# Two routing groups of 12 and 4 sequences instead of 10 and 6, in a new written-out order

## The chip, the cores and the metric

The kernel runs on one core of a Trainium2 chip. The metric is device time in microseconds for one launch. The core has TensorE (PE: matmuls; PEld: its weight loads), VectorE (DVE), ScalarE (ACT), GpSimd (POOL) and SyncE (SP), each working through its own queue in order. SyncE's queue issues most DMA transfers; GpSimd issues the indirect ones, whose rows go to computed addresses.

## The reference

One transformer layer on 16 sequences of 256 tokens, 128 values each, in float32. Attention has 16 heads of 8 values; the feed-forward layer has 8 experts, of which each token uses its best two.

```
qkv = x @ w_qkv;  Q, K = rope(Q), rope(K)
out = softmax(causal(Q @ K^T * 8**-0.5)) @ V            # 16 heads of 8
x   = layernorm(x + out @ w_proj + b_proj)
logits = x @ W_router + b_router;  best two per token, softmax over the two
for e in range(8):
    y = relu(x @ W1[e] + b1[e]) @ W2[e] + b2[e]          # 128 -> 512 -> 128
    final += y * w[:, e]                                 # 0 where e is not among the two
x   = layernorm(x + final)
```

## The kernel before, in words

**Recording and order.** The kernel first records operations ("ops"), each with its engine, the ops it waits for, and the tiles it holds. Then `Plan.emit` issues them in the order of the list `ORDER`, a written-out permutation of the ops' numbers. Because every engine works through its queue in order, this list fixes which instruction waits behind which on each engine, and on SyncE's and GpSimd's DMA queues too. It only has to respect the dependences. The costs and ranks that ops carry are not used once the list is there.

**Attention, one sequence at a time** (`attention`, sixteen of them, in the list interleaved with one another). TensorE transposes x (L780), makes Q and K with and without swapped halves (L793) and V together with a part of the router's logits (L838). VectorE applies the rotation (L802, L803, L810). ScalarE masks Q by head (L822). TensorE computes scores in three pieces (L871), into one PSUM buffer; ScalarE takes the exponential of each piece (L896, 1.88 us); GpSimd sets what is not causal to zero (L881, "mask", 1.1 us for two of them and 2.05 us for the third); TensorE multiplies by V (L912, "weighing", four ops: two long, two short). ScalarE copies the result (L925); the denominators go out by DMA, are inverted on VectorE (L938) and come back spread over the partitions; VectorE scales (L956); TensorE projects (L966, with the rest of the logits); VectorE adds x (L978) and takes the moments (L745, L746). Each pair of sequences is then normalized (ScalarE L752, L753; VectorE L757 to L759 and L996).

**Routing by chunks.** `CHUNKS` is a list of groups, each a list of chunks, each a number of sequences in their order. When a chunk's last sequence is normalized, `route` runs once for it: VectorE finishes the logits (L1077 to L1080) and picks the two best experts (L1067 to L1071, L1087 to L1090); TensorE counts, with two matmuls, how many tokens each expert has (L1096, L1097, "count"); ScalarE and VectorE make the weights (L1118, L1122 to L1125); VectorE turns counts into places (L1102 to L1112, "places"). Then GpSimd scatters the chunk's rows to these places in DRAM (`rows`), one indirect DMA per 128 tokens for the first expert and one for the second (L1140, "scatter"), so four per sequence; before the second half it writes new destinations (L1129, L1136). A chunk's places are computed from those of the chunk before in the same group.

**Expert blocks by groups.** When all chunks of a group have places, `finish` computes on VectorE how many blocks of 128 rows each expert has (L1191 to L1250), and SyncE pads the ends (L1042). Blocks of one expert's rows are then processed (`block`), either pairs of 256 rows or singles of 128. With T tiles of 128 tokens in the group there are T - 7 pairs, and 19 singles are run. A block loads its expert's first matrix (L1311, 256 KB) and its rows (L1315, 65 KB per 128 rows; the load waits for every scatter of the group), transposes the rows (L1323), copies them (L1332), multiplies (L1339), applies bias and ReLU on ScalarE (L1352), multiplies by the second matrix (L1360), adds the bias (L1370) and multiplies by the row's weight (L1379); GpSimd sends each 128 rows to their token's place in DRAM (`back`, L1387, "send").

**Combining.** When all blocks of a group are sent, `combine` fetches each sequence's two results (L1472, 256 KB), adds them, normalizes, and stores 128 KB (L1547). For the first group VectorE adds (L1488, L1489) and ScalarE scales (L1506). For the last group TensorE adds into PSUM (L1455, L1478) and GpSimd takes the inverse square root (L1496, L1497). Twelve matmuls that nothing reads (L1557) run on TensorE while the last group's sends land.

**Around the change.** Before, the groups have 10 sequences (chunks of 4, 4 and 2) and 6 (one chunk). Sequences are numbered from 0, chunks are numbered from 0 through both groups. Sequence 9 closes chunk 2 and sequence 15 closes chunk 3.

Of the kernel before, what the change touches and what calls it, by code (L numbers as in the profile page):

```python
# [287 lines left out]

CHUNKS = [[4, 4, 2], [6]]

WARM = 12

# [14 lines left out]


ORDER = """
7 0 45 46 1 14 47 9 15 12 2 11 50 29 81 6 3 4 22 10 13 48 49 5 82 51 52 24 56 54 53 86 17 21 19
23 87 30 57 93 55 59 94 16 58 88 18 60 20 25 83 121 65 31 61 26 157 84 85 122 123 124 91 66 89
68 158 44 90 62 92 63 159 160 161 126 32 95 96 125 127 197 128 162 133 132 64 163 131 98 69 99
67 198 70 71 8 97 130 72 33 101 104 129 102 100 164 233 169 103 234 134 73 74 141 75 142 166
105 106 107 108 135 143 167 136 27 109 76 170 202 203 204 168 28 110 138 165 139 199 111 137
144 209 656 200 201 140 208 112 171 145 206 146 147 172 655 77 148 177 173 149 113 178 78 150
179 151 238 79 210 239 207 174 152 34 205 80 175 114 653 176 235 180 658 115 116 236 211 237
117 118 240 212 181 182 183 184 185 153 186 35 244 245 214 243 215 187 188 213 273 120 119 220
154 657 217 216 242 155 274 246 278 279 659 275 276 241 218 250 219 280 251 277 221 309 310 281  # L320
284 189 222 223 247 282 190 248 311 156 252 224 249 191 192 193 253 37 285 225 256 314 283 254
286 312 290 194 195 196 664 313 291 226 255 315 316 257 385 386 665 258 662 227 259 260 261 293
666 36 390 391 392 318 317 294 319 320 667 672 670 287 262 671 228 288 654 387 668 295 263 349
321 292 322 669 388 389 289 350 326 678 296 297 298 327 264 680 229 673 395 323 324 328 679 299
300 265 301 394 354 355 351 352 329 302 353 230 356 325 231 393 232 332 303 396 330 405 661 333
406 38 674 675 676 331 357 266 267 358 360 399 334 335 400 336 425 677 41 268 361 304 397 337
338 339 426 340 407 402 398 362 359 401 427 537 681 403 686 269 430 538 366 408 305 367 428 429
431 404 409 410 432 434 685 270 363 435 688 364 411 271 306 682 436 433 542 369 341 307 412 413
308 543 370 342 684 368 539 544 343 344 540 549 42 442 365 372 373 371 374 541 345 443 414 663
546 346 347 272 348 545 415 39 375 416 439 690 550 376 577 377 691 692 378 379 548 440 689 444  # L330
437 438 461 547 578 445 683 694 462 695 446 441 693 463 448 698 417 380 696 697 687 447 554 418
703 464 555 702 465 419 381 420 706 699 551 43 552 466 467 468 556 469 470 579 382 449 383 471
384 421 705 580 700 557 422 450 451 558 582 583 472 452 581 481 482 613 584 589 590 553 453 614
560 478 40 561 704 479 423 587 615 701 475 424 454 716 717 718 720 721 719 559 483 588 616 455
722 707 713 723 734 735 480 712 739 501 476 738 586 742 585 477 724 725 456 727 728 562 563 617
660 564 597 743 744 618 473 565 737 619 620 598 591 745 746 747 474 484 485 592 709 711 726 593
710 486 487 978 566 567 594 502 488 506 621 489 507 595 508 624 596 729 715 623 457 568 490 491
503 622 762 775 630 504 505 631 736 492 510 512 708 731 732 730 599 714 748 600 625 626 601 513
627 628 458 633 511 602 741 509 634 569 740 603 604 733 605 493 518 570 514 571 572 629 632 749
494 635 519 459 515 516 636 637 638 639 460 606 776 517 763 979 520 607 495 496 497 640 641 521  # L340
929 777 778 498 522 608 524 980 779 780 981 642 523 500 643 782 982 525 750 499 781 609 526 527
930 983 528 931 783 784 785 764 610 928 644 765 611 767 529 530 645 531 769 893 612 932 933 766
532 646 934 647 648 880 879 768 787 935 649 892 751 752 984 985 986 969 786 770 936 650 652 533
754 534 771 756 651 772 894 535 536 987 573 881 773 753 895 897 814 882 574 576 575 1189 968
815 1190 896 755 899 774 898 757 758 867 900 759 883 1191 901 1192 1193 1194 937 1195 760 761
902 1197 884 866 903 1196 904 1223 1225 885 886 887 1226 888 889 868 1199 1201 1208 840 869 841
890 1205 891 816 970 971 972 973 1228 817 1232 1233 1234 939 1188 789 1209 819 818 974 975 821
938 820 976 1029 788 1207 977 1202 1227 1204 870 872 1019 871 1230 949 822 873 1198 874 842 823
824 875 876 877 825 826 843 1028 940 878 1030 941 1031 1505 845 847 844 1018 790 846 942 943
791 793 795 1200 1206 848 948 906 849 792 944 945 905 850 794 1049 946 1032 1020 852 1203 851  # L350
1033 1021 1048 796 797 798 947 950 1022 1023 988 951 989 952 953 799 800 1235 1034 1506 907
1035 1024 908 1050 1051 918 1025 1036 954 909 1037 1210 910 1089 919 1026 955 911 1214 1027
1088 1236 959 912 990 991 956 1052 957 1008 1212 913 914 1090 1009 1053 1054 1091 915 920 921
1217 1055 992 1092 993 922 1553 1056 994 995 958 917 802 916 1093 923 1094 1095 996 1096 801
1231 960 961 924 1010 962 925 926 1011 803 804 1012 1078 963 964 1222 1057 965 1237 854 1013
1508 853 1229 966 997 1213 1079 1220 1097 1221 805 806 807 855 808 998 1069 927 856 1014 1015
858 809 860 999 1080 857 1016 1224 1211 810 1218 1070 1081 1068 828 859 811 1017 967 1071 1082
827 1000 1083 861 1038 1001 862 1002 1072 812 813 1084 1058 1085 1039 1098 863 1003 1215 1004
1073 1005 829 865 830 1059 1099 1086 1074 1216 864 831 1075 1076 833 1006 1040 832 1219 1041
1042 1100 1393 834 1101 835 836 1043 1087 1060 1102 1061 1251 1062 837 1044 1077 1252 1007 1103  # L360
1104 1253 1063 1045 1394 1105 1064 1277 1254 838 1046 1484 1106 839 1065 1066 1255 1395 1278
1396 1257 1256 1047 1397 1483 1554 1485 1067 1374 1486 1258 1259 1107 1555 1398 1373 1265 1172
1156 1279 1280 1260 1399 1487 1264 1261 1263 1400 1401 1488 1281 1375 1282 1354 1376 1239 1132
1266 1262 1489 1267 1353 1283 1173 1140 1402 1490 1157 1174 1158 1238 1284 1491 1334 1148 1377
1492 1378 1333 1285 1286 1175 1268 1355 1159 1270 1176 1356 1177 1269 1271 1160 1343 1287 1364
1161 1379 1178 1179 1240 1288 1357 1289 1358 1162 1241 1380 1381 1141 1363 1142 1272 1273 1344
1143 1335 1242 1274 1244 1382 1133 1164 1243 1245 1336 1144 1290 1276 1291 1275 1145 1146 1359
1360 1361 1314 1365 1108 1366 1337 1134 1313 1362 1338 1246 1147 1149 1247 1135 1345 1248 1367
1163 1346 1368 1136 1137 1138 1424 1249 1339 1347 1150 1348 1292 1369 1340 1293 1295 1250 1341
1370 1371 1423 1180 1342 1151 1315 1165 1464 1316 1297 1463 1152 1153 1294 1296 1166 1154 1324  # L370
1323 1167 1349 1350 1425 1317 1351 1426 1318 1155 1414 1109 1298 1299 1372 1352 1465 1466 1168
1427 1413 1300 1110 1428 1433 1139 1301 1434 1319 1320 1325 1467 1169 1326 1429 1302 1321 1327
1415 1303 1322 1430 1468 1304 1431 1416 1453 1454 1328 1469 1432 1170 1417 1470 1471 1404 1472
1435 1436 1418 1403 1329 1330 1331 1332 1474 1181 1437 1305 1306 1438 1473 1182 1111 1419 1307
1183 1308 1420 1421 1455 1444 1456 1184 1439 1405 1457 1185 1458 1440 1441 1406 1443 1383 1384
1171 1112 1442 1113 1114 1309 1407 1115 1475 1116 1310 1476 1459 1408 1477 1460 1422 1461 1311
1445 1446 1462 1478 1409 1410 1411 1447 1448 1385 1124 1386 1479 1480 1481 1387 1388 1449 1389
1493 1509 1312 1494 1495 1412 1482 1450 1496 1497 1498 1499 1500 1390 1451 1186 1117 1510 1391
1187 1452 1501 1502 1392 1525 1503 1504 1507 1526 1539 1118 1125 1126 1119 1120 1127 1128 1546
1532 1540 1121 1122 1123 1129 1527 1528 1547 1541 1529 1542 1533 1130 1511 1512 1548 1549 1530  # L380
1543 1534 1544 1550 1535 1131 1518 1531 1551 1545 1519 1552 1513 1536 1520 1537 1514 1538 1515
1516 1517 1521 1522 1523 1524
"""


class Held:

    def __init__(self, pool, tag, shape, dtype, bufs):  # L390
# [64 lines left out]
def main_path(  # L455
# [24 lines left out]
    HW = HEADS // 2  # L480
    ROUTED = CHUNKS
    TC = max(max(g) for g in ROUTED) * NT
# [1192 lines left out]
```

## Time and profile before

| | |
|---|---|
| three timed runs | 379.85 us median (376.16, 379.85, 381.21) |
| profiled execution | 373.53 us, span 372.1 us, TensorE clock 0.981 |
| TensorE busy | 332.6 us (89%) |
| ScalarE, GpSimd, VectorE busy | 252.3, 218.0, 202.6 us |
| DMA | 46.5 MB, 125 GB/s over the span |
| counts of the four chunks on TensorE | first at 78.7, last at 213.2 us |
| first transpose of block rows | 185.28 us |
| last expert matmul ends | 349.55 us |

The profile is of one execution, with times from the start of its span. A line of a timeline gives start, length, engine, source line, operation, tiles, and in brackets how long the engine was idle before it and what released it. Granted clock is the share of TensorE's full speed that it was given in a stretch.

### The profile page before, as it was taken

The page shows a single profiled execution, that of the slowest core. Times are in us where ns is not written, and L with a number is a line of the kernel's source. Part 1 is how long each engine was busy: PE and PEld are TensorE (multiplying, and loading weights), DVE is VectorE, ACT ScalarE, POOL GpSimd, SP SyncE. Part 2 cuts the span into 40 slices and gives each one's busy share as a digit, 9 for nine tenths or more (in the row PEclk, how much of TensorE's full clock was granted, in tenths as well). Part 3 has the DMA queues.
Part 4 walks back from the last instruction along what each step waited for, and adds up shares of the span by engine and source line. Part 5 has one row for each costly group of instructions (what it writes and reads, how often), then busy time and mean ns, then how long its engine had stood idle before and what let it go on. Part 6 is the DMA issues. An engine that isn't in the chain of part 4 may idle for free.

```text
span 372.1 us, 9773 instructions
## 1 busy us (share of the span) xinstructions
PE 332.6 (89%) x2960; PEld 246.6 (66%) x2960; DVE 202.6 (54%) x731; ACT 252.3 (68%) x547; POOL 218.0 (59%) x252
## 2 busy tenths in 40 slices
PE   5999999979999696797999887999999899989980
PEld 3554555545566353444589767999898899989960
DVE  3440566786368879854567872143321267635551
ACT  2889778878788665677655453666666489978642
POOL 5155343446887489488822567777777446553632
PEclk9999999999999999699999999899999999999997
DMA  4100354131321221165345436665765687776472
GB/s 127 44 3 13 113 75 118 32 102 62 118 63 55 74 59 40 31 154 171 87 114 152 132 93 170 162 187 155 218 196 156 178 249 237 231 204 194 142 213 76
DMA packets 53098, 46.51 MB, mean 125 GB/s; under 512 B 14610, under 2 KB 39577, under 8 KB 53042
## 3 DMA queue, kind: packets, MB, share of 16 engines
q1 hardware_dynamic: 48626, 37.36, 37.5%
q0 software_dynamic: 4416, 8.47, 6.8%
q8 instruction: 27, 0.44, 0.5%
q14 instruction: 29, 0.24, 0.2%
HBM read 33.53 MB, written 12.67 MB: 124 GB/s over the span
## 4 chain that ended last, share of the span: by engine, by line
PE 55%; DVE 16%; ACT 11%; DMA 6%; issue 5%; POOL 4%; ACTq 0%; DVEq 0%; POOLq 0%; SPq 0%
PE m L1339 14%; PE m L1360 13%; PE sc L871 8%; PE ps_o L912 7%; ACT pr L896 7%; PE m L793 4%; PE m L966 3%; POOL rows L1140 2%; DMA rows_in<-rows 2%; DVE lg L1079 2%; DVE x_sb L996 2%; POOL pr L881 2%; PE ps_o L1557 1%; DMA out_dram<-yout 1%; PE m L1323 1%
## 5 line engine op out<-in xcount | busy, mean ns | idle before, releaser
L896 ACT ACTIVATE pr<-sc 128x2048 f32<-128x2048 f32 x48 | 90.1, 1877 | 26.8 <-PE sc L871 24.9
L1387 POOL DMA_INDIRECT back<-y,rows_in x74 | 72.8, 984 | 57.0 <-ACT y L1379 33.8
L881 POOL TENSOR_SCALAR_AFFINE_SELECT pr<-pr 128x1024 f32<-128x1024 f32 (+1 forms) x48 | 67.3, 1412 | 58.8 <-ACT pr L896 58.5
L1352 ACT ACTIVATE hT<-m,b_sb 128x128 f32<-128x128 f32 (+1 forms) x224 | 71.7, 407 | 21.8 <-PE m L1339 19.1
L1140 POOL DMA_INDIRECT rows<-x_sb,dest x64 | 65.3, 1020 | 22.7 <-issue 17.0
L1360 PE MATMUL m<-w_sb,hT 128*128 x592 | 75.5, 277 | 2.0 <-issue 1.1
L1339 PE MATMUL m<-rT,w 128*128 128x128 f32 (+1 forms) x448 | 75.8, 315 | 1.0 <-DVE rT L1332 0.4
L1360 PEld LDWEIGHTS m<-w_sb,hT 128*128 128x128 f32 x592 | 70.9, 192 | 4.8 <-ACT hT L1352 1.7
L1339 PEld LDWEIGHTS m<-rT,w 128*128 128x128 f32 x448 | 63.0, 194 | 5.9 <-DVE rT L1332 1.1
L871 PE MATMUL sc<-qTm,qk 32*128 32x512 f32 x384 | 55.7, 650 | 6.6 <-ACT pr L896 5.0
L912 PE MATMUL ps_o<-pr,va 128*32 128x128 f32 (+1 forms) x1024 | 49.9, 334 | 2.5 <-POOL pr L881 2.4
L1379 ACT ACTIVATE y<-y,rows_in 128x128 f32<-128x128 f32 x74 | 27.7, 401 | 30.4 <-DVE y L1370 30.1
L912 PEld LDWEIGHTS ps_o<-pr,va 128*32 128x32 f32 x1024 | 28.3, 111 | 29.4 <-issue 12.9
L1370 DVE TENSOR_TENSOR y<-m,b_sb 128x128 f32<-128x128 f32 (+1 forms) x56 | 18.7, 334 | 51.1 <-PE m L1360 41.8
L822 ACT ACTIVATE qTm<-qk,rows_sb 128x256 f32<-128x256 f32 x64 | 29.6, 506 | 1.8 <-DVE qk L810 1.8
L871 PEld LDWEIGHTS sc<-qTm,qk 32*128 32x128 f32 x384 | 15.2, 185 | 19.3 <-ACT pr L896 12.2
L793 PE MATMUL m<-xT,wqk_sb 128*128 128x256 f32 x64 | 22.5, 436 | 0.9 <-ACT xT L783 0.9
L802 DVE TENSOR_TENSOR part<-m,rope_sb 128x256 f32<-128x256 f32 x32 | 13.1, 410 | 18.6 <-PE m L793 18.1
L966 PEld LDWEIGHTS m<-wproj_sb,o 128*128 128x128 f32 x128 | 16.1, 190 | 7.2 <-issue 1.9
L956 DVE TENSOR_TENSOR o<-o,spread 128x512 f32<-128x512 f32 x16 | 13.7, 853 | 12.2 <-DMA spread<-recs 12.2
L793 PE MATMUL m<-xT,wsw_sb 128*128 128x256 f32 x64 | 20.0, 395 | 0.0
L1332 DVE COPY rT<-m 128x128 f32<-128x128 f32 (+1 forms) x32 | 10.6, 340 | 16.1 <-PE m L1323 14.2
(152 smaller groups left out, 362.6 us busy)
## 6 DMA issues: line engine op xcount, KB each, us to landing
w<-in_L_ffn_W_dram SPq DMA_DIRECT2D x56, 256.0 KB
spread<-recs SPq DMA_DIRECT2D x16, 256.0 KB
ys<-back SPq DMA_DIRECT2D x16, 256.0 KB
rows_in<-rows SPq DMA_DIRECT2D x38, 65.0 KB
rows_in<-rows SPq DMA_DIRECT2D x18, 130.0 KB
x<-in_L_attn_x_dram SPq DMA_DIRECT2D x16, 128.0 KB
w_sb<-in_L_ffn_W_dram SPq DMA_DIRECT2D x8, 256.0 KB
out_dram<-yout SPq DMA_DIRECT2D x16, 128.0 KB
```

The costliest lines, as they stand in the source:

```text
L793: nc.tensor.matmul(ps.get()[:, c, :], w[:, s, :], xT.get(), start=True, stop=True)
L822: lambda j=j: nc.scalar.activation(qTm.get()[:, j, :], qk.get()[:, 0], AF.Copy, scale=rows_sb[:, j : j + 1]),
L871: nc.tensor.matmul(ps.get()[:, g], qk.get()[rg, 1, ts(kt, P)], qTm.get()[rg, js, kt * P : S], start=True, stop=True,)
L881: nc.gpsimd.affine_select(out=pr.get()[:, :, :, 0:P], in_=pr.get()[:, :, :, 0:P], compare_op=ALU.is_ge, fill=0.0, base=0, pattern=[[0, GRO ...
L896: lambda pr=pr, ps=ps: nc.scalar.activation(pr.get(), ps.get(), AF.Exp),
L912: nc.tensor.matmul(pso.get()[ts(g, 32), t, kt * P : S], va_t[:, kt, 2 * g + t].rearrange("p u c -> p (u c)")[:, 16 * u : 16 * u + 32], pr. ...
L1140: nc.gpsimd.indirect_dma_start(out=g.rows[:, :], out_offset=bass.IndirectOffsetOnAxis(ap=g.dest[:, k, t - g.t0 : t - g.t0 + 1], axis=0), i ...
L1339: nc.tensor.matmul(ps_h[i].get()[:, c, :], w.get()[:, ts(i * per + c, P)], rT.get()[:, 0 : n * P], start=True, stop=True,)
L1352: nc.scalar.activation(hT.get()[:, at, 0 : n * P], ps_h[i].get()[:, c, :], AF.Relu, bias=bias)
L1360: nc.tensor.matmul(ps_y.get()[:, i, :], hT.get()[:, c, i * P : (i + 1) * P], w2_sb[:, bass.ds(e, 1), c, :].rearrange("p o d -> p (o d)"), ...
L1379: nc.scalar.activation(y.get()[:, i, :], y.get()[:, i, :], AF.Copy, scale=rows_in.get()[:, i, D + 1 : DX],)
L1387: put = nc.gpsimd.indirect_dma_start(out=g.back[:, :], out_offset=bass.IndirectOffsetOnAxis(ap=rows_in.get()[:, i, D : D + 1].bitcast(I32) ...
```

## The change

The first group now has 12 sequences in chunks of 4, 4, 2 and 2, and the last group has 4 sequences in one chunk. So there are five chunks instead of four; sequence 9 closes chunk 2, sequence 11 closes chunk 3, and sequence 15 closes chunk 4. The first group has 24 tiles (17 pairs, 19 singles), the last 8 (1 pair, 19 singles); before it was 20 (13, 19) and 12 (5, 19). Since the numbers of the ops change, the whole list `ORDER` is replaced by another one.

```diff
-CHUNKS = [[4, 4, 2], [6]]
+CHUNKS = [[4, 4, 2, 2], [4]]
...
 ORDER = """
-7 0 45 46 1 14 47 9 15 12 2 11 50 29 81 6 3 4 22 10 13 48 49 5 82 51 52 24 56 54 53 86 17 21 19
...
-1543 1534 1544 1550 1535 1131 1518 1531 1551 1545 1519 1552 1513 1536 1520 1537 1514 1538 1515
-1516 1517 1521 1522 1523 1524
+7 0 45 1 15 46 50 9 10 29 3 14 2 21 51 52 47 30 22 81 5 82 4 31 48 49 55 54 56 20 86 83 87 53
...
+1548 1559 1560 1561 1562 1537 1552 1553 1554 1555 1538 1539 1540 1541
```

The numbers say little by themselves. Around the last count of the first group, the queues are as follows (s10 is sequence 10).

```
TensorE, before, from chunk 2's count to the first block: count; s12 transpose; s13 two short
  weighings; s14 score; s15 projection; s11 V; s14 score; s11 four weighings; s14 score;
  s12 two projections; s15 score; s14 weighing; s15 V; s14 weighing; s12 V; s15 score;
  s10 output projection; s15 score; s14 two short weighings; s12 score; s13, s11 output
  projections; s12 score; s15 four weighings; s12 score; first transpose of block rows
TensorE, after, from chunk 2's count to the first block: count; s12 short weighing; s10 output
  projection; s15 score; s11 output projection; s14 V, projection; s15 score; s14 projection;
  s13 V, score; s15 weighing; s13 score; s15 weighing; chunk 3's count; s15 two short weighings;
  s13 weighing, score; s14 score; s13 weighing; s12 output projection; s13 two short weighings;
  s14 two scores; s15 output projection; s14 four weighings; first transpose of block rows
GpSimd, before, from chunk 2's destinations: 3 scatters of chunk 2, 2 of chunk 1, 1 of 2; s14 mask;
  1 of 1; s14 mask; second destinations; 2 of 1, 3 of 2; s14 mask; 1 of 1, 1 of 2; s15 and s12 masks
GpSimd, after, from chunk 3's destinations: 1 scatter of chunk 1, 4 of chunk 3; s13 mask; 1 of 2;
  second destinations; 2 of 3, 1 of 2, 2 of 3; s14 three masks; first send
VectorE, after, from chunk 2's choice to chunk 3's: reciprocal of s11; s13 rotation; chunk 2's
  weights; s13 rotation; s10 scaling; chunk 2's places; s11 scaling; reciprocal of s12; s10, s11
  residuals and moments; s14 rotation; s10 and s11 normalized; chunk 3's logits and choice
```

The transposes of block rows come, in both lists, when most attention work has been queued on TensorE: before, four weighings of s12 and the output projections of s14, s15 and s12 stand behind the first of them; after, the output projections of s13 and s14. In the last group's stage the stores (L1547) of eight sequences of the first group stand behind the last block's loads in SyncE's queue, before those of five.

## The prediction

> **What bounds the kernel now.** I read the page's busy shares and its chain first, then a table of stretches, then the timelines around the one long gap of TensorE, and last the end of the span. "Sequence 12" below is the thirteenth of the sixteen, "chunk 2" the third chunk of the first group.
>
> ```profile
> span 372.1 us, 9773 instructions
> PE 332.6 (89%) x2960; PEld 246.6 (66%) x2960; DVE 202.6 (54%) x731; ACT 252.3 (68%) x547; POOL 218.0 (59%) x252
> PE 55%; DVE 16%; ACT 11%; DMA 6%; issue 5%; POOL 4%; ACTq 0%; DVEq 0%; POOLq 0%; SPq 0%
> ```
>
> TensorE works for 332.6 of 372.1 us and is over half of the chain. The change keeps its work, so the time is that work plus TensorE's idle time, 39.5 us. The table of stretches says where that idle time lies (columns: stretch, its length, busy time and instructions of each engine, granted TensorE clock, DMA share, GB/s):
>
> ```profile
> 125.00:146.40 21.40, 19.58 (x187) 10.55 (x186) 18.38 (x54) 14.65 (x17) 16.64 (x14) 1.00 0.20 56
> 146.40:150.70 4.30, 0.09 (x4) 0.00 (x0) 3.85 (x15) 0.00 (x0) 3.35 (x5) 0.91 0.06 17
> 150.70:156.00 5.30, 5.27 (x46) 3.05 (x46) 4.51 (x24) 3.75 (x6) 1.81 (x3) 0.50 0.06 16
> 156.00:185.30 29.30, 25.77 (x309) 14.81 (x305) 15.67 (x61) 21.86 (x28) 24.52 (x24) 0.99 0.52 138
> 290.00:349.60 59.60, 57.66 (x462) 55.02 (x463) 31.51 (x132) 47.61 (x156) 30.03 (x31) 1.00 0.74 214
> 349.60:372.10 22.50, 12.60 (x54) 9.55 (x52) 10.19 (x51) 8.38 (x23) 7.52 (x14) 0.92 0.47 132
> ```
>
> Between 146.4 and 150.7 TensorE does nothing, and for the next 5.3 us its clock is 0.50. From 290 to 349.6 it is busy for 57.7 of 59.6. After 349.6 comes the tail. The timelines of VectorE, GpSimd, TensorE and SyncE's queue show what the gap was (start, length):
>
> ```profile
> 141.79 4.63 DVE L1079 TENSOR_TENSOR lg<-lg,rstd_sb 128x32 f32<-128x32 f32 x1
> 150.59 0.15 DVE L1090 TENSOR_TENSOR d<-m,m 128x4 f32<-128x4 f32 x1
> ...
> 142.36 4.00 POOL L881 TENSOR_SCALAR_AFFINE_SELECT pr<-pr 128x2048 f32<-128x2048 f32 x2
> 155.38 1.01 POOL L1140 DMA_INDIRECT rows<-x_sb,dest  x1 [0.96 <-DVE qk L810]
> 177.62 1.13 POOL L1140 DMA_INDIRECT rows<-x_sb,dest  x1 [0.30 <-issue]
> ...
> 150.73 0.64 PE L1096 MATMUL m<-hot,before 128*128 128x32 f32 x2 [4.24 <-DVE hot L1089]
> 185.28 0.44 PE L1323 MATMUL m<-ident,rows_in 128*128 128x128 f32 x2
> ...
> 181.45 2.14 SPq L1315 DMA_DIRECT2D rows_in<-rows  x3
> ```
>
> The count of chunk 2 (L1096) stands in TensorE's queue until VectorE has chosen the experts, and everything queued behind it waits too. From that count it is 34.5 us to the transpose of the first expert block (185.28): places on VectorE, scatters on GpSimd until 178.75, loads issued at 181.45, TensorE at 185.28. TensorE had 29 us of attention to fill this with.
>
> **The change part by part.** *Work that stays.* A group of T tiles has T-7 pairs and 19 single blocks run. Before: 13 and 5 pairs; after: 17 and 1. Both make 18 pairs, 38 singles, 74 sends and 64 scatters, so block work on TensorE, ScalarE and GpSimd and the weight loads are worth nothing either way.
>
> *One more chunk.* A fifth count adds 0.8 us on TensorE, and some 8 us of small VectorE operations. VectorE is 54% busy, so only their place matters.
>
> *The first block starts later.* It now waits for chunk 3, sequences 10 and 11. I counted TensorE's order and priced the pieces from the trace (transpose 0.4, projection 0.97, V 0.63, score 1.07, weighing 1.0 or 0.47, output projection 1.0). Ahead of the first block stand two long and two short weighings, one output projection and one count more than before: 2.0 + 0.9 + 1.0 + 0.8 = 4.7 us, which is work taken from behind it. With unchanged idle time the first block would start at 185.3 + 4.7 = 190.0. Only what exceeds 190.0 is loss. There are three steps to it.
>
> 1. Chunk 2's count is placed 6.5 us of work later than before: 146.4 + 6.5 = 153. VectorE chose at 150.6 before, with as much queued in front, so this count doesn't wait.
>
> 2. Between the counts of chunks 2 and 3 TensorE has 12 us of work. VectorE must, in its order: finish sequence 13's rotation, chunk 2's weights and the scaling of sequence 10's output (4.2 us), places of chunk 2 (2.4), sequence 11's scaling and a reciprocal (1.0), wait for its projection, then residuals and moments (3.2), rotation and normalization (2.8), and choose chunk 3's experts. It reaches the choice at about 166. The choice costs 17 operations at 0.19 = 3.5 us when undisturbed (chunk 1, twice as wide, took 4.8), or 9.3 as in chunk 2 before, whose L1079 took 4.63 us instead of 0.19 while GpSimd masked. So the count runs at 170 to 175.5; I take the middle, 172.5, since two masks of sequence 13 are queued on GpSimd at just that place. TensorE, also held 2.8 us by sequence 10's scaling, arrives at 168.
>
> 3. From chunk 3's count to its first scatter: 4.65 (150.73 to 155.38). GpSimd then has four scatters, a mask of sequence 13, one scatter, the second destinations, and five scatters: 10 x 1.28 + 1.1 + 0.8 = 14.7. The last scatter ends 19.4 us after the count. From there 2.7 to the first load and 3.8 to the transpose, as in the lines: 25.9. Sequence 14's three masks are queued behind all of these scatters on GpSimd and end 23.7 us after the count, so its weighings, which TensorE has ahead of the first block, end at about the same time. TensorE has only 13.6 us of work in these 25.9, where before it had 29 in 34.5.
>
> The first block then starts at 172.5 + 25.5 = 198, between 195.5 and 201.5: 8 us lost, 5.5 to 11.5. The gap of before is inside this comparison already. A long idle stretch ends with a slow clock: before, 5.3 us at 0.50, which is 2.6 us lost. After, part of it falls beside the waits for masks; I take 1.5 of 0 to 2.6.
>
> The Trainium skill, "SBUF — State Buffer", section "Who interferes with whom", says that VectorE and GpSimd share a port pair as an exclusive lock held for a whole instruction, and that a tensor_tensor with both inputs in SBUF contends with GpSimd's reads. The 4.63 us row, ending as the masks do, agrees. By that rule alone a two-sequence choice beside two masks would be at the late end, and the sum 3 us higher than mine; by the undisturbed row it would be 2.5 lower.
>
> *The expert stage.* The last group's routing has over 70 us of block work in front of it, as before; nothing. Its blocks are now 19 singles and 1 pair, about 40 us of TensorE work after the last block of the first group, against 50, and the first group's results come back in it: 12 sequences x 384 KB, not 10. With some 17 blocks of 385 KB still to be loaded and sent that is 11 MB in 36 us, 310 GB/s. The trace moved 214 at a share of 0.74, which full would be 289 (estimate). Excess 2.4 us, but the queue order lets eight output stores slip behind the last block: I take 1, of 0 to 6. This cover also hides two more combinations on VectorE and ScalarE; without it they cost about 2.4 us each.
>
> *The tail.* Four sequences instead of six. The outputs' last step (L1506) on ScalarE:
>
> ```profile
> 363.44 0.81 ACT L1506 ACTIVATE yout<-sc,off,rstd 128x128 f32<-128x128 f32 x2 [0.28 <-PE sc L1478]
> ...
> 365.89 0.81 ACT L1506 ACTIVATE yout<-sc,off,rstd 128x128 f32<-128x128 f32 x2 [0.33 <-DMA out_dram<-yout]
> ```
>
> These are the fourth and the sixth: 2.45 us gained. Four sequences of the first group are then on VectorE first (2.4 us each, some 8 us after the last block), and the first sums came 7.6 us after it before, so this nearly balances: -2.5, of -3 to 0.
>
> Sum: +8 + 1.5 + 1 - 2.5 = **+8 us**. The profiled execution took 373.53 us, below the lowest timed run (376.16) and 6.3 below the median; 373.5 + 8 = 381.5 there, so 379.85 + 8 = **388** on the scale of the runs, 2.1% up. About 2% (7.6 us) is what a measurement of this kernel can tell from no change.
>
> **The rivals.**
> *A. The long chain stays covered, and the kernel is faster.* One mechanism: chunk 2's count, moved later, no longer waits, so the 4.2 us gap and its 2.6 us of slow clock go, and nothing replaces them: 4.2 + 2.6 + 2.5 (tail) - 0.8 = 8.5 gained, 371. For it speaks that step 1 is sound by itself. It decides if the chain from chunk 2's count to the first block (172.5 + 25.5 - 153 = 45 us) fits into the 25.6 us of work there, that is if VectorE and GpSimd ran some 19 us ahead. GpSimd's window speaks against it: from 85.8 to 178.8 it was busy for 72.7 of 93 us, with 0.3 us between most of 40 scatters, and now has 48 scatters.
> *B. The new wait costs about what the old one did.* The choice is undisturbed (170) and the scatters left over from chunk 2 are already out, so that the first block starts at 193 or 194: +3.5, tail -2.5, DMA +1: 382, no change.
> *C. The forecast and a last stage bound by transfers.* The 310 GB/s aren't reached, block loads queue behind returning results, 6 us instead of 1, and the choice is at its late end (+3): 397.
> That the change does not do what it says can be excluded for the work (the counts above); that the order fills the gap with other attention work can't be: little is left, of sequences 13 and 14.
>
> **How the numbers follow.** Forecast 0.38 (383 to 393), B 0.30 (378 to 386), C 0.18, A 0.14. The range of 8 in 10 cuts A and C in half: 374 to 399. Faster by over 2%: most of A, 0.11. Slower by over 2% (387.5): C and a good half of the forecast with a little of B, 0.47. Within 2%: 0.42.
>
> **What would show it.** Step 2: in the changed profile TensorE idle before the count of the fourth chunk, released by VectorE, some 5 us. Step 3: about 25 us from that count to the first transpose of block rows, with idle time before weighings, released by GpSimd's masks, and a clock near 0.5 there. Expert stage: TensorE over 95% busy with DMA shares above 0.8 in the last 50 us. Tail: about 20 us from the last expert matmul to the end. I am wrong if the first block starts near 190 or sooner, or if the early attention, whose order is new everywhere, has much less idle time than the 11.5 us of before's first 125.

## The result, and the profile after

The changed kernel is **slower**: 383.86 us (median of 4 runs, 382.82 to 384.70), against 378.15 for the kernel before (4 runs, 376.16 to 381.21). The ratio on record is 1.027, with a 95% interval of 1.023 to 1.031; the quotient of the two medians is 1.015. Ratios are taken over undisturbed runs (the kernel before took 373.5 us in its profile and about 373 beside e5 to e11), and where e1 to e4 and e12 ran, every kernel was slower (the kernel before took 426.7 and 428.7 us, although e9 to e11 ran on the chip of e1 to e4), so of those five the ratios can be set beside the others, but not the times and dates. The profiled executions took 383.93 and 373.53 us, 10.4 us apart.

The page of the changed kernel (span; busy time of each engine):

```profile
span 382.2 us, 9807 instructions
...
PE 334.9 (88%) x2952; PEld 247.4 (65%) x2952; DVE 221.5 (58%) x768; ACT 253.9 (66%) x552; POOL 216.2 (57%) x251
```

TensorE's busy time is up by 2.3 us only, and its idle time from 39.5 to 47.3. VectorE is up by 18.9 us, of which the fifth chunk was priced at 8. Stretches from count to count, and from the last count to the first block (columns as in the table of stretches before):

```profile
83.10:126.85 43.75, 35.23 (x374) 20.39 (x370) 34.08 (x98) 29.64 (x42) 31.46 (x29) 1.00 0.21 64
126.85:163.61 36.76, 31.61 (x331) 17.82 (x331) 28.14 (x81) 23.87 (x33) 26.25 (x26) 0.91 0.23 71
163.61:180.45 16.84, 14.27 (x116) 8.54 (x116) 13.88 (x52) 10.39 (x14) 10.50 (x11) 0.90 0.19 58
180.45:208.92 28.47, 19.10 (x213) 10.34 (x213) 18.68 (x69) 11.08 (x14) 21.14 (x21) 0.82 0.42 123
```

The single 4.2 us gap of before is gone. In its place TensorE idles 8.5, 5.2, 2.6 and 9.4 us in four stretches, three of them with a clock below full. The timelines of TensorE, VectorE, GpSimd and SyncE's queue name the waits:

```profile
126.85 0.69 PE L1096 MATMUL m<-hot,before 128*128 128x64 f32 x2 [2.98 <-DVE hot L1089]
163.61 0.41 PE L1096 MATMUL m<-hot,before 128*128 128x32 f32 x2 [2.65 <-DVE qk L810]
180.45 0.41 PE L1096 MATMUL m<-hot,before 128*128 128x32 f32 x2 [0.57 <-DVE hot L1089]
188.05 2.09 PE L871 MATMUL sc<-qTm,qk 32*128 32x512 f32 x8 [2.39 <-ACT qTm L822]
198.23 2.06 PE L871 MATMUL sc<-qTm,qk 32*128 32x512 f32 x8 [2.06 <-ACT pr L896]
204.49 4.49 PE L912 MATMUL ps_o<-pr,va 128*32 128x256 f32 x64 [2.23 <-POOL pr L881]
208.92 0.44 PE L1323 MATMUL m<-ident,rows_in 128*128 128x128 f32 x2
...
155.66 3.79 DVE L1068 TENSOR_TENSOR key<-rest,m 128x32 f32<-128x32 f32 x1
176.08 2.74 DVE L1071 TENSOR_TENSOR hot<-key,k 128x32 f32<-128x32 f32 x1
156.30 3.10 POOL L881 TENSOR_SCALAR_AFFINE_SELECT pr<-pr 128x2048 f32<-128x2048 f32 x2
...
205.17 2.70 SPq L1315 DMA_DIRECT2D rows_in<-rows  x3
```

Chunks 1 and 2 hold TensorE up; chunk 3's count hardly does (0.57). Chunk 2's choice is again stretched beside masks: L1068 takes 3.79 us instead of 0.19, and ends as GpSimd's two masks end. The count of chunk 2 was released not by this choice itself, which ended at 160.4, but by the rotation of sequence 13 (L810), which stands behind the choice on VectorE; the count takes its PSUM buffer from the same pool as the projections that L810 reads. In the last stretch TensorE waits 5.9 us for ScalarE (1.42, 2.39 and 2.06) and 3.3 us for masks (1.08 and 2.23), and sequence 14's weighings run at half clock up to the first block.

| us from the start of the span | before | predicted | after |
|---|---|---|---|
| chunk 2's count | 150.7 | 153 | 163.6 |
| chunk 3's count (two sequences, first group) | - | 172.5 | 180.5 |
| first block | 185.3 | 198 | 208.9 |
| last expert matmul ends | 349.6 | 360 | 361.9 |
| end of the span | 372.1 | 380 | 382.2 |

The first block comes 23.6 us later, not 12.7. From the first block to the end of the span it is 173.3 us instead of 186.8, which gives 13.5 back, where my terms gave 6.2 (4.7 moved work and 2.5 tail, less 1). The difference of the two, 10.1, is the loss; my sum was 12.7, plus 1.5 for the slow clock, less 6.2, so 8.

### The profile page after: what moved, and what is told of

It reads as the page before. It is cut to its first block, busy times and chain, and to the rows that moved or that the text cites. A ratio compares the mean times of both kernels' runs of the same rounds, so it can differ in the third digit from the quotient of the medians.

```text
span 382.2 us, 9807 instructions
## 1 busy us (share of the span) xinstructions
PE 334.9 (88%) x2952; PEld 247.4 (65%) x2952; DVE 221.5 (58%) x768; ACT 253.9 (66%) x552; POOL 216.2 (57%) x251
## 5 line engine op out<-in xcount | busy, mean ns | idle before, releaser
L896 ACT ACTIVATE pr<-sc 128x2048 f32<-128x2048 f32 x48 | 90.0, 1876 | 33.3 <-PE sc L871 29.8
L1360 PE MATMUL m<-w_sb,hT 128*128 x592 | 76.3, 278 | 2.5 <-DVE newton L757 0.9
L1339 PE MATMUL m<-rT,w 128*128 128x128 f32 (+1 forms) x448 | 72.8, 310 | 0.5 <-DVE rT L1332 0.4
L871 PE MATMUL sc<-qTm,qk 32*128 32x512 f32 x384 | 57.7, 671 | 13.1 <-ACT pr L896 9.1
L912 PE MATMUL ps_o<-pr,va 128*32 128x128 f32 (+1 forms) x1024 | 53.5, 348 | 6.8 <-POOL pr L881 5.4
L912 PEld LDWEIGHTS ps_o<-pr,va 128*32 128x32 f32 x1024 | 29.4, 115 | 31.7 <-issue 13.9
L871 PEld LDWEIGHTS sc<-qTm,qk 32*128 32x128 f32 x384 | 15.7, 192 | 28.4 <-ACT pr L896 18.0
L822 ACT ACTIVATE qTm<-qk,rows_sb 128x256 f32<-128x256 f32 x64 | 30.5, 505 | 4.1 <-DVE qk L810 4.1
L966 PEld LDWEIGHTS m<-wproj_sb,o 128*128 128x128 f32 x128 | 17.4, 205 | 9.1 <-issue 3.4
L793 PEld LDWEIGHTS m<-xT,wqk_sb 128*128 128x128 f32 x64 | 10.6, 197 | 16.9 <-issue 8.0
L966 PE MATMUL m<-wproj_sb,o 128*128 128x136 f32 x128 | 20.1, 304 | 1.1 <-DVE o L956 1.1
```

What stands on the lines that cost most here:

```text
L793: nc.tensor.matmul(ps.get()[:, c, :], w[:, s, :], xT.get(), start=True, stop=True)
L822: lambda j=j: nc.scalar.activation(qTm.get()[:, j, :], qk.get()[:, 0], AF.Copy, scale=rows_sb[:, j : j + 1]),
L871: nc.tensor.matmul(ps.get()[:, g], qk.get()[rg, 1, ts(kt, P)], qTm.get()[rg, js, kt * P : S], start=True, stop=True,)
L896: lambda pr=pr, ps=ps: nc.scalar.activation(pr.get(), ps.get(), AF.Exp),
L912: nc.tensor.matmul(pso.get()[ts(g, 32), t, kt * P : S], va_t[:, kt, 2 * g + t].rearrange("p u c -> p (u c)")[:, 16 * u : 16 * u + 32], pr. ...
L966: nc.tensor.matmul(ps_p.get()[:, q, :], o.get()[:, t, ts(q, P)], wproj_sb[:, t, :], start=(t == 0), stop=(t == 1),)
```

## The experiments

The theory under test (**chain**): the first block cannot start before the last chunk in front of it has been chosen, placed and scattered and TensorE's last attention work has its masks, and its start sets the end. Its rival (**count**): the loss is made earlier, by counts that wait in TensorE's queue, with the slow clock behind them. A second question is whether the grouping or the new attention order is to blame. Beside e5 to e8 the kernel before took 373.9 us, beside e9 to e11 372.9. Ratios are always against the kernel before, measured beside the run.

**e10, counts moved back in the changed kernel.** TensorE's queue:

```diff
-chunk 1's count
 V of sequence 10; two short weighings of 8; transpose of 15; score of 11
+chunk 1's count
...
-chunk 2's count
 short weighing of sequence 12; score of 15
+chunk 2's count
```

> The edit of e2 once more (chunk 1's count behind five pieces of attention work, chunk 2's behind two), because the chip of e1 to e4 was 12% slower. Count theory: 5 to 8 us below the changed kernel. Chain theory: 0 to 3 us below it, and idle time ahead of the first block that is released by GpSimd, VectorE or the row loads.

Measured: ratio 1.027 (1.024 to 1.031), exactly the changed kernel's. TensorE and ScalarE:

```profile
129.01 1.33 PE L871 MATMUL sc<-qTm,qk 32*128 32x512 f32 x8 [3.03 <-ACT pr L896]
162.21 1.14 PE L871 MATMUL sc<-qTm,qk 32*128 32x512 f32 x8 [1.52 <-ACT pr L896]
205.89 0.44 PE L1323 MATMUL m<-ident,rows_in 128*128 128x128 f32 x2 [0.18 <-DMA rows_in<-rows]
...
126.98 0.21 ACT L1118 ACTIVATE d<-d 128x8 f32<-128x8 f32 x1 [3.85 <-DVE d L1090]
127.10 1.86 ACT L896 ACTIVATE pr<-sc 128x2048 f32<-128x2048 f32 x1
```

Both counts now run without a wait, but TensorE waits for the PSUM buffer of the score put ahead of it, which ScalarE's exponential (L896) frees: 3.03 us at the first place, where the count had waited 2.98, and 1.52 at the second, where it had waited 2.65. In ScalarE's queue this exponential stands behind the chunk's weights (L1118), which wait for VectorE's choice, 3.85 us for chunk 1 and 4.08 for chunk 2. So the early wait was not taken away: the late choice reaches TensorE through ScalarE's queue. Chunk 2's count comes at 163.85, as before the edit at 163.61. The profiled execution is the fastest of the four by 2.8 us, so its first block, 3.0 us sooner than in the changed kernel, can't be put down to the edit. The forecast of the count theory (5 to 8 us below) falls: the places of the counts are not the cause. What the early lateness itself costs, e10 doesn't show. The same kernel had run earlier as e2:

> The changed kernel, with chunk 1's count moved behind five pieces of attention work and chunk 2's count behind two. Count theory (the loss is the waits of 2.98 and 2.65 us ahead of these two counts with the slow clock behind them, which the new order brought, not the grouping): 5 to 8 us below the changed kernel, so 0 to 3 us above before. Chain theory (chunk 3's choice, places and scatters set the first block): 0 to 3 us below the changed kernel, first transpose of block rows not before 206 us.

There the ratio was 1.016 (1.009 to 1.022), which is above before too, but some 1% below that of e10 for the same kernel; the changed kernel was not measured beside it, so it says no more.

**e5, keeping the clock up.** Matmuls that nothing reads, ahead of the work that waits:

```diff
             def weigh(r=r, kt=kt, t=t, pr=pr):
+                for _ in range(8 if (b, r) == (14, 0) else 0):
+                    nc.tensor.matmul(pso.get()[:, 0, 0:P], ident, ident, start=True, stop=True)
```

and likewise ahead of sequence 14's first score.

> The changed kernel with matmuls that nothing reads put on TensorE where it stands idle: 12 of 64 columns ahead of chunk 1's count, 8 of 128 columns ahead of the first score of sequence 14 and 8 ahead of its first weighing, 2 to 3 us at each place. The instructions wait for the same things as before, only the clock stays up. If the slow clock is a cost of its own (10.1 us of TensorE's busy time ahead of the first block are slow clock, against 3.3 in the kernel before), the time falls by 3 to 6 us below the changed kernel. If VectorE's and GpSimd's chain sets when the first block starts, it falls by 0 to 2 us, and the first block stays within 2 us of where it is.

Of these, the twelve ahead of chunk 1's count were not issued (the condition read a variable that had moved on when the operation ran), so the run tests the two places of sequence 14. Measured: 1.027 (1.022 to 1.033), no change. The stretch from chunk 3's count to the first block, and the first block:

```profile
182.37:210.02 27.65, 19.88 (x245) 13.24 (x245) 18.70 (x69) 11.68 (x15) 21.23 (x21) 0.94 0.44 125
...
210.02 0.44 PE L1331 MATMUL m<-ident,rows_in 128*128 128x128 f32 x2 [0.82 <-DMA rows_in<-rows]
```

The clock there rose from 0.82 to 0.94, the stretch fell by only 0.8 us, and the first block then waited 0.82 us for its rows. The slow clock in that stretch costs at most these 0.8 us: the rows are not there sooner. What the slow clock behind chunk 1's count costs was not tested.

**e6 and e7, masks of the last four sequences narrowed**, in the changed kernel and in the one before:

```diff
-                    out=pr.get()[:, :, :, 0:P],
-                    in_=pr.get()[:, :, :, 0:P],
+                    out=pr.get()[:, :, :, 0 : P if b < 12 else 1],
+                    in_=pr.get()[:, :, :, 0 : P if b < 12 else 1],
```

> The changed kernel, with GpSimd's masks of sequences 12 to 15 narrowed to one column of 128 (the causal mask of these sequences is left out). Some 16 us of GpSimd work go, nearly all of it between chunk 1's and chunk 3's scatters. If the chain through GpSimd (masks in the scatters' queue, and VectorE's choice stretched beside them) delays the first block as the chain theory says, the first block starts 8 to 15 us earlier and the time falls by 6 to 12 us below the changed kernel, to before's or under it. If TensorE's own waits in the attention order cost the time, it falls by 0 to 3 us.

> The same narrowing in the kernel before (the causal mask of sequences 12 to 15 is left out). Chain theory: the masks cost here only the gap of chunk 2, 2 to 6 us, less than in the changed kernel. If masks cost both kernels the same, they say nothing about the change.

Measured: 1.010 (1.007 to 1.014) for the changed kernel, some 6 us below it, at the lower end of the chain theory's 6 to 12; 0.995 (0.992 to 0.999) for the one before, 1.7 us (2 to 6 on record). VectorE and TensorE of the changed kernel without these masks:

```profile
153.25 0.19 DVE L1068 TENSOR_TENSOR key<-rest,m 128x32 f32<-128x32 f32 x1
...
201.55 0.44 PE L1323 MATMUL m<-ident,rows_in 128*128 128x128 f32 x2 [0.90 <-DMA rows_in<-rows]
```

L1068 is back at 0.19. Chunk 2's count comes at 159.4 without a wait, chunk 3's at 175.1, the first block at 201.6: 4.3, 5.3 and 7.4 us sooner (8 to 15 was on record for the last). VectorE's busy time falls by 13 us here, and by 4.6 in the kernel before. So over 4 of the 10 us lost are these masks, which in the changed order stand beside two choices and cost twice: in GpSimd's queue and in VectorE's time. The runs don't separate these two.

**e8, chunks 2 and 3 as one chunk of four.**

```diff
-CHUNKS = [[4, 4, 2, 2], [4]]
+CHUNKS = [[4, 4, 4], [4]]
```

> The changed kernel's order and groups, with chunks 2 and 3 made one chunk of four sequences (8 to 11), placed where chunk 3 was: one count, one choice, one set of places less, but all 16 scatters of four sequences behind the last choice and not 8. Chain theory (the first block follows the last chunk's scatters): the first block starts 6 to 8 us later than in the changed kernel, and the time is 4 to 8 us above it. If the additional chunk's own cost is what slows the changed kernel, the time is 2 to 5 us below it.

Measured: 1.045 (1.040 to 1.049), 6.6 us above the changed kernel, as the chain theory has it. TensorE and GpSimd:

```profile
177.79 0.43 PE L1096 MATMUL m<-hot,before 128*128 128x64 f32 x2 [0.21 <-DVE hot L1089]
211.82 5.34 PE L912 MATMUL ps_o<-pr,va 128*32 128x256 f32 x64 [10.99 <-POOL pr L881]
...
209.59 4.14 POOL L881 TENSOR_SCALAR_AFFINE_SELECT pr<-pr 128x1024 f32<-128x1024 f32 x3
```

One chunk's work is saved, and the count comes 2.7 us sooner than chunk 3's did. But between the last chunk's first destinations and sequence 14's masks GpSimd has 17 scatters instead of 11, TensorE waits 10.99 us for these masks instead of 2.23, and the first block starts at 217.1, 8.2 us later. This is step 3 of the prediction, made large.

**e11, chunk 2's count moved back in the kernel before.** This was meant to close the old gap:

```diff
-chunk 2's count
 transpose of sequence 12; two short weighings of 13; score of 14
+chunk 2's count
```

> The edit of e1 once more (chunk 2's count in the kernel before behind 2.5 us of attention work), for the same reason. Count theory: 4 to 6 us below before. Chain theory: within 1.5 us of before, with the gap moved to what waits for VectorE next, the score that needs sequence 14's rotated Q.

Measured: 1.018 (1.011 to 1.025): 6.7 us slower, which neither theory had. ScalarE and TensorE:

```profile
151.23 0.20 ACT L1118 ACTIVATE d<-d 128x4 f32<-128x4 f32 x1 [5.43 <-DVE d L1090]
153.50 0.89 ACT L822 ACTIVATE qTm<-qk,rows_sb 128x256 f32<-128x256 f32 x2
...
154.44 2.09 PE L871 MATMUL sc<-qTm,qk 32*128 32x512 f32 x8 [6.46 <-ACT qTm L822]
156.47 0.64 PE L1096 MATMUL m<-hot,before 128*128 128x32 f32 x2
```

The late choice is waited for in two queues. ScalarE's weights (L1118) stood 5.43 us for it, and behind them the masking of sequence 14's Q, which the score needs that I had put ahead of the count. The count ran 5.7 us later than before, the first block 3.9 us later, and the span of the profiled execution, the fastest of the four, was 3.2 us longer. The same kernel, run earlier as e1:

> The kernel before, with chunk 2's count moved in TensorE's queue behind a transpose of sequence 12, two short weighings of sequence 13 and a score of sequence 14 (2.5 us of work). If what is lost is the wait itself, as the count theory says, the 4.2 us gap at 146.4 and the 2.6 us of slow clock behind it mostly go, and the time is 4 to 6 us below before. If the chain theory holds (choice, places, scatters on VectorE and GpSimd set when the first block starts, and TensorE's attention work only fills the time), the gap goes but reappears later as idle time, the first transpose of block rows stays at 184 to 187 us, and the time is within 1.5 us of before.

There the ratio was 1.011 (1.005 to 1.017), the same sign. So the old gap was VectorE's lateness, and could not be closed by moving TensorE's count alone.

**Grouping or order? e3, e4, e9, e12.** Four attempts to have one without the other. e3: the new attention order with groups 10 and 6. e4: the old attention order with groups 12 and 4. e9 and e12: the changed kernel with only this:

```diff
-CHUNKS = [[4, 4, 2, 2], [4]]
+CHUNKS = [[4, 4, 2], [2, 4]]
```

e12 also moves VectorE's block tables and chunk 2's last scatters, after what e9 showed.

> The groups of before (10 and 6), with the attention work, the chunks 0 to 2 and the set-up in the changed kernel's order on every engine, and the rest in before's. If the grouping costs the time (a fourth chunk ahead of the first block), the first block starts at 187 to 195 us and the time is within 3 us of before. If the new order of the attention costs it, the first block starts at 198 us or later and the time is 5 to 10 us above before.

> The groups of the change (12 and 4), with the attention work and chunks 0 to 2 in before's order on every engine, and the rest (chunk 3's routing, blocks, combining) placed as the changed kernel has it. If the grouping costs the time, the first block starts at 196 to 212 us and the time is 6 to 14 us above before. If the new attention order costs it, the first block starts at 188 to 194 us and the time is within 3 us of before.

> The changed kernel's attention order with the five chunks 4, 4, 2, 2, 4 as they are, but the groups are again 10 and 6: sequences 10 and 11 go to the last group, so the first block no longer waits for chunk 3; chunk 3's choice and count stand behind sequence 14's rotation and last score, its scatters behind sequence 14's masks; the blocks keep the changed kernel's places. Chain theory: the first block starts at 192 to 198 us, not 209, and the time falls by 5 to 10 us below the changed kernel. If the waits of the new attention order cost the time and the grouping does not, it stays within 3 us of the changed kernel although the first block starts sooner.

> As e9 (changed kernel's attention order, chunks 4, 4, 2, 2, 4, groups of 10 and 6), with what spoiled e9 taken away: the 8 us of VectorE work that finds the blocks of the first group stand behind sequence 14's rotation and not ahead of sequence 11's scaling, chunk 2's last scatters stand ahead of sequence 13's masks, chunk 3's choice, count and scatters stand behind the first blocks, and the last chunk's routing is advanced by up to four blocks. Chain theory: no chunk 3 ahead of the first block, so it starts at 193 to 199 us (that is TensorE's own work behind chunk 2's count at 163 us), and the time is 5 to 10 us below the changed kernel. If the attention order alone costs the time, the first block starts as soon, but the time stays within 3 us of the changed kernel.

Measured: 1.066, 1.059, 1.094 and 1.052, all above the changed kernel's 1.027, and every one outside both of its forecasts; none is a clean answer. The first blocks came at 212.9, 227.7, 216.4 and 219.5 us, of which only e9's can be set beside 185.3 and 208.9 (one and the same kernel has its first block at 204.1 in e1 and at 189.1 in e11). e4 is the plainest. Its work up to chunk 2's count is that of before, and then the stretch from chunk 3's count to the first block is:

```profile
206.07:227.74 21.67, 5.11 (x45) 4.19 (x45) 9.38 (x53) 0.79 (x2) 8.23 (x10) 0.50 0.40 110
```

TensorE works 5.1 of 21.7 us, at half clock: the fourth chunk with nothing behind it to fill its chain. In e9, 8 us of VectorE work that finds the blocks stood ahead of sequence 11's scaling (TensorE idled 5.27 us for that), and the first block came at 216.4. In e12 that was moved, and the first group's last scatter ended at 191.5, yet the first block came 28 us behind it. GpSimd, TensorE and SyncE's queue:

```profile
212.82 4.59 POOL L881 TENSOR_SCALAR_AFFINE_SELECT pr<-pr 128x1024 f32<-128x1024 f32 x3 [10.56 <-ACT pr L896]
215.03 4.49 PE L912 MATMUL ps_o<-pr,va 128*32 128x256 f32 x64 [3.09 <-POOL pr L881]
219.45 0.44 PE L1323 MATMUL m<-ident,rows_in 128*128 128x128 f32 x2
...
213.47 2.16 SPq L1315 DMA_DIRECT2D rows_in<-rows  x3
```

The first block does not wait for rows here. TensorE has sequence 14's four weighings ahead of it, these wait for their masks, and the masks for sequence 14's exponentials on ScalarE. The load of the first rows, 22 us behind the last scatter, stands in SyncE's queue behind sequence 13's denominators, for which the queue waited 8.1 us (L934, on ScalarE's copy L925); it would be the next gate. e9 has the same picture: its first block waits for nothing but TensorE's own order, and the load goes out at 209.84, 8.6 us behind the last scatter (2.7 in the kernel before). So in the new order three things meet at the first block: chunk 3's scatters, sequence 14's attention on TensorE and ScalarE, and SyncE's queue with sequence 13's denominators. Taking away one leaves the others. How much a good order for 10 and 6 with chunks of 2 and 4 in the last group would give stays open, and with it the split of the loss between grouping and order.

**What all runs share.** From the first block to the end of the span, without e1 to e4 and e12:

| kernel | groups | first block | from there to the end |
|---|---|---|---|
| before | 10, 6 | 185.3 | 186.8 |
| e7, masks narrowed | 10, 6 | 184.4 | 186.2 |
| e11, count moved | 10, 6 | 189.1 | 186.2 |
| e9, split | 10, 6 | 216.4 | 188.0 |
| after | 12, 4 | 208.9 | 173.3 |
| e5, clock kept up | 12, 4 | 210.0 | 173.6 |
| e10, counts moved | 12, 4 | 205.9 | 172.2 |
| e6, masks narrowed | 12, 4 | 201.6 | 172.1 |
| e8, merged chunk | 12, 4 | 217.1 | 172.7 |

The second column of times depends on the groups, within 2 us, while the first varies by 33. In these nine runs the start of the first block sets the end. Groups of 12 and 4 pay once the first block comes less than some 13.5 us later than before; here it came 23.6 later. No edit that left the computation whole beat the kernel before.

## Why the prediction was right, and where its steps were not

The direction, the size (388 forecast on the scale of 379.85, so +8 us; +10.1 measured between the spans) and the mechanism held: a later first block, only in part paid back behind it. That the sum came out so near is luck, by two errors that nearly cancel: with the 1.5 us for slow clock the first block came 9.4 us later than forecast, and the time behind it was 7.3 us shorter.

*Step 1 failed.* Chunk 2's count came at 163.6, not 153, and it waited. I had added 6.5 us of work and taken the rest of the attention as it was. Up to this count TensorE idled 20.9 us instead of 17.6, so that the 4.24 us that I let vanish came back with 3.3 more; with some 3 us of slow clock (busy time is up by 9.56, not by 6.5) that is the 10.6. My own sign for being wrong, much less idle time early, came out the other way: 15.7 us up to 126.85 after, 11.5 up to 124.47 before. e10 and e11 show that these waits do not hang on the counts' places: VectorE's choice is late, and what waits for it stands in several queues. e6 gives 4.3 of the 10.6 us to the masks (3.1 of idle time, the rest clock).

*Step 2 half held.* From count to count it took 16.8 us, not 19.5. The choice was stretched as foreseen (L1071 took 2.74 us), but TensorE's wait was 0.57, not 5: counted from chunk 2's count, VectorE was through 2.7 us sooner than forecast, and TensorE arrived 1.3 us later (16.3 us, not 15).

*Step 3 held in the main*: 28.5 us from chunk 3's count to the first block, against 25.5 to 25.9; the last scatter ended 21.5 us after the count (19.4 forecast), the loads went out 24.7 us after it (22.1), with waits for masks (1.08 and 2.23 us) and a clock of 0.82. e8 showed the scatters ahead of the masks as the part that grows. What I had not seen is ScalarE, for which TensorE waits longer there (5.9 us) than for the masks. Sequence 14's last exponential ended at 202.21, only 0.3 us after the last scatter (201.93), so without the scatters its mask could hardly have come sooner, which fits with e9 and e12. Nor had I seen that SyncE's queue holds back the loads: in e6 they went out 5.3 us behind the last scatter, after L943 (195.70), and the first block waited 0.90 us for its rows.

*The expert stage was mis-sized.* I wrote +1 us beside 4.7 us of moved work; measured from the first block to the last expert matmul are 153.0 us instead of 164.3, so 6.6 us less than the moved work explains. No transfer bound came (rival C): DMA shares reached 0.84, with TensorE busy 18.6 of 20 us. The gain lies early, behind the first blocks. Before, in two stretches of 20 us:

```profile
205.30:225.30 20.00, 17.43 (x113) 15.01 (x112) 15.31 (x75) 10.73 (x31) 11.91 (x14) 1.00 0.40 113
225.30:245.30 20.00, 18.03 (x130) 16.87 (x129) 4.78 (x20) 9.94 (x31) 15.19 (x16) 0.91 0.65 177
```

and after, as far behind the first block:

```profile
228.90:248.90 20.00, 20.00 (x139) 18.56 (x138) 11.17 (x58) 13.02 (x37) 13.85 (x15) 1.00 0.52 146
```

Before, TensorE idles 4.5 us in these two stretches and loses some 1.8 to a clock of 0.91 (after, it is busy for all of this stretch and of the next); VectorE, busy 15.3 of 20, has the routing of six sequences there, and after that of four only 11.2. That the smaller last chunk is the cause is argued from these rows, not shown by a run.

*The tail held*: 20.3 us from the last expert matmul to the end, 20 forecast. *Rival A* (covered, faster) fell on its own condition, and *rival B* too (first block at 193 or 194).

The rule of the Trainium skill ("SBUF — State Buffer", "Who interferes with whom"), that a tensor_tensor with both inputs in SBUF contends with GpSimd's reads, agrees with the trace in kind: one of 0.19 us took up to 3.79 beside masks, and 0.19 again where these were narrowed. In size neither bound of the prediction, 3.5 and 9.3 us, was met: the choices of chunks 2 and 3 took 8.5 and 6.2 us, and 3.6 and 3.7 in e6.

## What to carry to other kernels

When work is moved in front of a gate, price the gate by its own chain and by every queue that reaches it (the loads' queue too), and then check the idle time ahead of it: an order that is new everywhere has no old idle time to inherit. Look for one date that all later work hangs on; here the time from the first block to the end hardly depended on anything but the grouping. Where an engine waits for a late result, find all queues in which something waits for it, before moving one.

## What the runs showed that was not expected

- 2.98 us without a matmul was enough for some 6.5 us at half clock (126.85 to 133.4 in the changed kernel); in e10, after 3.03 us idle, the clock was 0.70 over 5.7 us, so half for some 3.4. In e8 even 1.37 us was followed by a clock of 0.62 (four weighings from 97.40 took 4.49 us), where the same wait in the changed kernel left it at 1.00 (2.81 us from 96.85). The Trainium skill ("TensorE: Matmul & The Clock Gate", "Part 1: The HAM clock gate") has the slow clock after at least one idle window of about 3.4 us, and the window free-running. That like waits end differently fits with a free-running window; that 1.37 us can be enough does not fit with a whole idle one, and the measurement decides.
- Narrowing the masks of four sequences took 13 us off VectorE's busy time in the changed kernel and 4.6 in the one before, although VectorE ran the same instructions. So busy time in a profile holds waiting, and a busier VectorE can be a stretched one.
- The late choice of a chunk was waited for on TensorE (the count), on ScalarE (the weights, with an exponential behind them) and, through the rotation behind it, by a PSUM buffer. Moving the count alone closed none of these gaps (e10, e11).
